# FFN order in an attention and FFN block: a gate's two parts behind the next gate's Silu, the next block's integers, projection and norms spread over both wide layers

## The chip, the cores and the metric

The kernel runs on one core of a Trainium2 chip. The metric is the device time of one execution in microseconds, the median of several runs. One further execution was taken with the hardware profiler; all views of the profile come from that one.

The engines of a core are named as the profile names them: PE (TensorE, matmuls; PEld are its weight loads), DVE (VectorE), ACT (ScalarE), POOL (GpSimd), SP (SyncE, which here only issues DMAs). They run side by side and wait for each other through semaphores.

## The reference, cut to what matters

One transformer block with the norm behind each part, on x of 4096 rows of 256 columns. The attention projects integers of 4 bits with ternary weights, and gives y; its last projection, again with integers, is computed in the kernel next to the FFN. The FFN is five linear layers with ternary weights `w` and a scale `s` for each output:

```python
def _tlin(x, w, s):
    return jnp.einsum('bsi,oi->bso', x, w) * s
# attention's end: quant4(y) @ ternary_weight(Wo_w).T
x = _layernorm(x + attention(x))
h = silu(_tlin(x, w1_w, w1_s)) * _tlin(x, w2_w, w2_s)      # 256 -> 1024, the gates
h = gelu(_tlin(h, h1_w, h1_s))                             # 1024 -> 1024, wide layer h1
h = gelu(_tlin(h, h2_w, h2_s))                             # 1024 -> 1024, wide layer h2
x = _layernorm(x + _tlin(h, w3_w, w3_s))                   # 1024 -> 256, the last layer
```

`quant4` divides each row by its largest absolute value, multiplies by 7, rounds and clips.

## The kernel before

**Stages.** A short stage quantizes x and projects it. The attention then takes some 3.1 ms of the span; its output y goes to DRAM (`y_dram`, eight blocks of 512 rows). The FFN comes last. `ffn(True)` (L718) is what runs with these weights, under `tc.manual_schedule()` (L853): each engine gets its instructions in the order in which the code writes them, and nothing is moved.

**The FFN's blocks.** The outer loop (L807) takes eight blocks b of 512 rows. Activations lie transposed, 128 features on the partitions by 512 rows. The weights are exact in fp32r, the matmuls' input type, and the activations are not; so each activation is split into two parts, its rounded value and the rest. `parts` (L725) makes them: a copy that rounds (L727, on ACT for the gates and on DVE for the wide layers) and a subtraction on DVE (L729). `product` (L733) forms 128 outputs for the 512 rows: one PSUM bank, with two matmuls (L745) for each 128 inputs.

**A block's layers**, in the order of PE:

- The gates (L810): for each o of 8, `gates` (L764) makes two products of 4 matmuls, then Silu of the first on ACT (L768), then on DVE the second product times its scale times the Silu (L770), then the two parts into `ha`.
- h1 (L820): for each o of 8, `hidden` (L776) makes one product of 16 matmuls, which reads `ha` in the order of k, both parts of each; then Gelu on ACT (L779), then the two parts into `hb`, both on DVE.
- h2 (L839): the same from `hb`.
- The last layer (L843): two products of 16 matmuls, each scaled on ACT into `fT` (L786).

**What is woven in between.** `add_up` (L788) transposes the last layer's result of block b-1 back and adds it to `xs[b-1]`. It stands behind gates 0 and 1 of block b. The closing norm of block b-1 has three steps (`layernorm_steps`, L181): `measure` (four pairs of BATCH_NORM on DVE, L189 and L190), `root` (a Sqrt on ACT, L193) and `scale` (a reciprocal and four scalings on DVE, L197 and L199). Then `store` (L799) issues the output's DMA on SP.

The next block's front (`front_steps`, L210) has seven steps. Calling it issues the load of `yb` on SP (L214). The steps are: `integers` (`quantize`, L117: eight DVE instructions on the row block), `transposed` (eight transposes on PE, L224, and a copy on ACT, L226), two projections (four matmuls on PE, L232; two DVE instructions, L241; two POOL additions, L244), and then `measure`, `root` and `scale` of that block's first norm. `transpose_x` (L756) at last transposes the normalized block, and makes its parts, for the gates of block b+1. `load_x` (L178) loads x for block b+2 on SP; three buffers of `xs` rotate, so that it goes into the buffer that `store` of block b-1 reads.

**What sets the order before.** In the gates: `measure` of block b-1 behind gate 2, and the call of `front_steps` for b+1 behind gate 4. In h1: front steps 0 to 4 behind products 0 to 4; front `root`, the closing norm's `root` and `scale`, and front `scale` behind product 5; the store behind product 6; `load_x` behind product 7. In h2: `transpose_x` behind product 1.

**Buffers.** PSUM has eight banks in one rotation (`psC`, L706), a bank for each product and each transpose. Silu and Gelu write into `gate`, three buffers in rotation, which `fT` shares. `h` has two buffers, `qtmp`, `qint`, `qT` and `yb` one each.

Of the kernel before, what the change touches and what calls it, by code (L numbers as in the profile page):

```python
# [29 lines left out]
NC = DH // P  # L30
# [7 lines left out]
def attn_ffn_kernel(  # L38
# [22 lines left out]
    nc = tc.nc  # L61
# [104 lines left out]
    def load_weights(sb, src, k0):  # L166

        n = min(sb.shape[1], 2)
        for k in range(0, sb.shape[1], n):
            nc.gpsimd.dma_start(  # L170
                out=sb[:, k : k + n, :],
                in_=src[(k0 + k) * P : (k0 + k + n) * P, :].rearrange("(k p) o -> p k o", p=P),
            )

    x_bufs = [xpool.tile([P, BT, D], F32, name=f"xs{i}") for i in range(3)]
    xs = {b: x_bufs[b % 3] for b in range(NT // BT)}

    def load_x(b):  # L178
        nc.sync.dma_start(out=xs[b], in_=x_t[:, ts(b, BT), :])
# [78 lines left out]
    with ExitStack() as actx:  # L258
# [371 lines left out]
        with tc.manual_schedule():  # L630
# [33 lines left out]
            w2_sb, h1_sb, h2_sb = [None, None], [None, None], [None, None]  # L664
# [37 lines left out]
    with ExitStack() as fctx:  # L702
        wpool2 = fctx.enter_context(tc.tile_pool(name="wpool2", bufs=1))
        hpool = fctx.enter_context(tc.tile_pool(name="hpool", bufs=2))
        tmp = fctx.enter_context(tc.tile_pool(name="tmp", bufs=2))
        psum = fctx.enter_context(tc.tile_pool(name="psC", bufs=8, space=PSUM))  # L706

        h2_sb[0] = kpool.tile([P, NC // 2, DH], F32R, name="h2a", tag="kT")
        h2_sb[1] = wpool2.tile([P, NC // 2, DH], F32R, name="h2b")
        w3_sb = wpool2.tile([P, NC, D], F32R, name="w3_sb")  # L710
        for i in range(2):
            load_weights(h2_sb[i], h2T, i * NC // 2)
        load_weights(w3_sb, w3T, 0)

        def bank(shape, dt):
            return psum.tile(shape, dt, name="ps_mm")

        def ffn(split):  # L718


            np_ = 2 if split else 1
            dt = F32R if split else F32
            nb = NT // BT

            def parts(dst, k, g, eng):  # L725

                eng(dst[:, k, 0, :], g)  # L727
                if split:
                    nc.vector.tensor_tensor(  # L729
                        dst[:, k, 1, :], g, dst[:, k, 0, :].bitcast(F32), ALU.subtract  # L730
                    )

            def product(w, o, src):  # L733
                ps = bank([P, 512], F32)
                sbs, dram_w = w
                n = dram_w.shape[0] // P
                if not split:
                    wo = tmp.tile([P, NC, P], F32, name="wo", bufs=1)[:, :n, :]
                    nc.sync.dma_start(
                        out=wo, in_=dram_w[:, ts(o, P)].rearrange("(k p) o -> p k o", p=P)  # L740
                    )
                for k in range(n):
                    sb, ks = sbs[k * len(sbs) // n], k % (n // len(sbs))
                    for i in range(np_):
                        nc.tensor.matmul(  # L745
                            ps,
                            lhsT=sb[:, ks, ts(o, P)] if split else wo[:, k, :],
                            rhs=src[:, k, i, :],
                            start=(k == 0 and i == 0),
                            stop=(k == n - 1 and i == np_ - 1),  # L750
                        )
                return ps

            xTs, fTs = {}, {}

            def transpose_x(b):  # L756
                xTs[b] = tmp.tile([P, 2, np_, BT * P], dt, name="xT", bufs=1)
                for k in range(2):
                    ps = bank([P, 512], F32)
                    for i in range(BT):  # L760
                        nc.tensor.transpose(ps[:, ts(i, P)], xs[b][:, i, ts(k, P)], ident)
                    parts(xTs[b], k, ps, nc.scalar.copy)

            def gates(b, o, ha):  # L764
                pa = product(((w1_sb,), w1T), o, xTs[b])
                pb = product((w2_sb, w2T), o, xTs[b])
                gate = tmp.tile([P, BT * P], F32, name="gate", bufs=3)
                nc.scalar.activation(gate, pa, AF.Silu, scale=scales["s1"][:, o : o + 1])  # L768
                g = gate if split else ha[:, o, 0, :]
                nc.vector.scalar_tensor_tensor(  # L770
                    g, pb, scales["s2"][:, o : o + 1], gate, ALU.mult, ALU.mult
                )
                if split:
                    parts(ha, o, g, nc.scalar.copy)

            def hidden(w, sc, o, ha, hb):  # L776
                ps = product(w, o, ha)
                g = tmp.tile([P, BT * P], F32, name="gate", bufs=3) if split else hb[:, o, 0, :]
                nc.scalar.activation(g, ps, AF.Gelu, scale=scales[sc][:, o : o + 1])  # L779
                if split:  # L780
                    parts(hb, o, g, nc.vector.tensor_copy)

            def last_layer(b, o, ha):
                ps = product(((w3_sb,), w3T), o, ha)
                fTs[o] = tmp.tile([P, BT * P], F32, name="fT", tag="gate", bufs=3)
                nc.scalar.activation(fTs[o], ps, AF.Copy, scale=scales["s3"][:, o : o + 1])  # L786

            def add_up(b, o):  # L788
                pt = bank([P, 512], F32)
                for i in range(BT):  # L790
                    nc.tensor.transpose(pt[:, ts(i, P)], fTs[o][:, ts(i, P)], ident)
                nc.vector.tensor_tensor(
                    xs[b][:, :, ts(o, P)],
                    xs[b][:, :, ts(o, P)],
                    pt.rearrange("p (i d) -> p i d", d=P),
                    ALU.add,
                )

            def store(b):  # L799
                nc.sync.dma_start(out=out_t[:, ts(b, BT), :], in_=xs[b])  # L800

            def hlayer():
                return hpool.tile([P, NC, np_, BT * P], dt, name="h")

            transpose_x(0)
            ends = None
            for b in range(nb):  # L807
                fronts = None
                ha = hlayer()
                for o in range(NC):  # L810
                    gates(b, o, ha)
                    if b and o < 2:
                        add_up(b - 1, o)
                    if b and o == 2:
                        ends = layernorm_steps(xs[b - 1])
                        ends[0]()
                    if o == 4 and b + 1 < nb:
                        fronts = front_steps(b + 1, bank)
                hb = hlayer()
                for o in range(NC):  # L820
                    hidden((h1_sb, h1T), "hs1", o, ha, hb)
                    if o < 5 and fronts:
                        fronts[o]()
                    if o == 5:

                        if fronts:
                            fronts[5]()
                        if ends:
                            ends[1]()
                            ends[2]()  # L830
                        if fronts:
                            fronts[6]()
                    if o == 6 and ends:
                        store(b - 1)
                        ends = None
                    if o == 7 and b + 2 < nb:
                        load_x(b + 2)
                ha, hb = hb, hlayer()
                for o in range(NC):  # L839
                    hidden((h2_sb, h2T), "hs2", o, ha, hb)  # L840
                    if o == 1 and b + 1 < nb:
                        transpose_x(b + 1)
                for o in range(2):  # L843
                    last_layer(b, o, hb)
            for o in range(2):
                add_up(nb - 1, o)
            for f in layernorm_steps(xs[nb - 1]):
                f()
            store(nb - 1)

        differs = nc.values_load(flag[0:1, 0:1], min_val=0, max_val=1)
        with tc.If(differs == 0) as cmp:
            with tc.manual_schedule():  # L853
                ffn(True)
        with cmp.Else():
            with tc.manual_schedule():
                ffn(False)
# [51 lines left out]
```

## Time and profile before

| What | us |
|---|---|
| median of 3 runs | 3928.08 |
| lowest and highest run | 3924.14 to 3934.04 |
| the profiled execution | 3924.8 |
| span of the profile, first to last instruction | 3923.0 |
| first matmul of the FFN's gates, from the span's start | 3179.05 |

The profile is one execution. A stretch of the trace is named by microseconds from the span's start. In the timeline each line gives the start, the duration, the engine, the line of the code, the operation with output<-input, the shape and the count of instructions merged. In brackets stands how long the engine was idle before it and what released it. A matmul's end is modelled, so successive matmuls overlap in the timeline; their starts are what to compare. The granted clock (PEclk) is a share of TensorE's full clock.

### The profile page before, as it was taken

The page shows a single profiled execution, that of the slowest core. Times are in us where ns is not written, and L with a number is a line of the kernel's source. Part 1 is how long each engine was busy: PE and PEld are TensorE (multiplying, and loading weights), DVE is VectorE, ACT ScalarE, POOL GpSimd, SP SyncE. Part 2 cuts the span into 40 slices and gives each one's busy share as a digit, 9 for nine tenths or more (in the row PEclk, how much of TensorE's full clock was granted, in tenths as well). Part 3 has the DMA queues.
Part 4 walks back from the last instruction along what each step waited for, and adds up shares of the span by engine and source line. Part 5 has one row for each costly group of instructions (what it writes and reads, how often), then busy time and mean ns, then how long its engine had stood idle before and what let it go on. Part 6 is the DMA issues. An engine that isn't in the chain of part 4 may idle for free.

```text
span 3923.0 us, 62034 instructions
## 1 busy us (share of the span) xinstructions
PE 3794.9 (97%) x25163; PEld 2161.9 (55%) x25163; DVE 3074.1 (78%) x5286; ACT 2385.0 (61%) x2694; POOL 420.6 (11%) x769
## 2 busy tenths in 40 slices
PE   4999999999999999999999999999999999999998
PEld 3555555555555555555555555555555557777776
DVE  6988888888888888888888888888888834444443
ACT  1467766766676776776666766766767753333332
POOL 6100011011100110011001100111000010000000
PEclk7799999999999999999999999999999999999999
DMA  2000000000000000000000000000100020000000
GB/s 56 1 3 2 8 8 8 8 8 8 8 8 8 8 8 8 8 8 8 8 8 8 8 8 8 8 2 24 45 2 19 2 72 17 17 17 17 17 6 12
DMA packets 59943, 49.36 MB, mean 13 GB/s; under 512 B 35232, under 2 KB 54304, under 8 KB 59648
## 3 DMA queue, kind: packets, MB, share of 16 engines
q1 hardware_dynamic: 55360, 33.11, 3.1%
q0 software_dynamic: 4288, 12.21, 1.0%
q8 instruction: 199, 3.26, 0.3%
q14 instruction: 96, 0.79, 0.1%
HBM read 36.92 MB, written 8.39 MB: 12 GB/s over the span
## 4 chain that ended last, share of the span: by engine, by line
PE 88%; DVE 8%; ACT 2%; issue 1%; DMA 0%; POOL 0%; SPq 0%; ACTq 0%; POOLq 0%; DVEq 0%
PE av L554 26%; PE sc L532 24%; PE ps L491 20%; PE ps_mm L745 13%; DVE mx L499 3%; PE ps L575 2%; DVE gate L770 1%; PE ps L519 1%; PE ps L462 1%; PE ps L416 1%; ACT gate L768 1%; DVE differ L616 0%; ACT h L727 0%; DVE qtmp L127 0%; DVE h L729 0%
## 5 line engine op out<-in xcount | busy, mean ns | idle before, releaser
L499 DVE TENSOR_REDUCE mx<-ps 128x1 f32<-128x512 f32 x4096 | 2558.6, 684 | 371.2 <-PE ps L491 353.9
L540 ACT ACTIVATE pr<-sc 128x1024 f32<-128x1024 f32 x2048 | 2012.6, 1024 | 906.5 <-PE sc L532 902.3
L491 PEld LDWEIGHTS ps<-kT,qT 64*128 64x128 f32 x4096 | 563.3, 185 | 987.1 <-DVE mx L499 636.6
L554 PE MATMUL av<-pr,v_all 128*32 128x512 f32 x8192 | 1092.8, 605 | 0.0
L491 PE MATMUL ps<-kT,qT 64*128 64x512 f32 x4096 | 1077.8, 470 | 9.2 <-DVE mx L499 8.4
L532 PE MATMUL sc<-mrow,minus 64*128 64x512 f32 x4096 | 867.5, 407 | 3.2 <-ACT pr L540 3.0
L532 PE MATMUL sc<-qT,kT 64*128 64x512 f32 x4096 | 834.2, 391 | 0.0
L532 PEld LDWEIGHTS sc<-qT,kT 64*128 64x128 f32 x4096 | 408.5, 185 | 78.7
L532 PEld LDWEIGHTS sc<-mrow,minus 64*128 64x128 f32 x4096 | 402.3, 186 | 76.7 <-ACT pr L540 19.3
L554 PEld LDWEIGHTS av<-pr,v_all 128*32 128x32 f32 x8192 | 161.6, 108 | 259.2 <-issue 255.9
L779 ACT ACTIVATE gate<-ps_mm,sc_hs 128x512 f32<-128x512 f32 x128 | 88.2, 689 | 326.3 <-PE ps_mm L745 301.7
L727 DVE CAST h<-gate 128x512 fp32r<-128x512 f32 x128 | 54.6, 427 | 266.8 <-ACT gate L779 266.6
L612 POOL CAST wround<-xs 128x1024 fp32r<-128x1024 f32 x22 | 22.9, 1039 | 1442.4 <-DMA xs<-in_h1T 512.6
L729 DVE TENSOR_TENSOR h<-gate,h 128x512 fp32r<-128x512 f32 x192 | 133.0, 692 | 48.3 <-ACT h L727 43.9
L745 PE MATMUL ps_mm<-h,h1b 128*128 128x512 f32 x512 | 140.9, 403 | 17.4 <-ACT h L727 12.7
L745 PE MATMUL ps_mm<-h,h1a 128*128 128x512 f32 x512 | 140.9, 421 | 0.0
L745 PE MATMUL ps_mm<-h,h2a 128*128 128x512 f32 x512 | 127.2, 390 | 0.0
L745 PEld LDWEIGHTS ps_mm<-h,h1b 128*128 128x128 f32 x512 | 98.2, 192 | 51.9 <-ACT h L727 20.6
L745 PE MATMUL ps_mm<-h,h2b 128*128 128x512 f32 x512 | 126.5, 389 | 0.0
L745 PEld LDWEIGHTS ps_mm<-h,h1a 128*128 128x128 f32 x512 | 102.2, 203 | 21.7
L745 PEld LDWEIGHTS ps_mm<-h,h2b 128*128 128x128 f32 x512 | 96.1, 188 | 20.0
L745 PEld LDWEIGHTS ps_mm<-h,h2a 128*128 128x128 f32 x512 | 95.6, 188 | 19.6
(147 smaller groups left out, 1978.0 us busy)
## 6 DMA issues: line engine op xcount, KB each, us to landing
xb<-in_x SPq DMA_DIRECT2D x8, 512.0 KB, 3.9
y_dram<-yu SPq DMA_DIRECT2D x64, 64.0 KB, 1.8
xs<-in_h1T SPq DMA_DIRECT2D x8, 512.0 KB, 4.0
xs<-in_h2T SPq DMA_DIRECT2D x8, 512.0 KB, 3.9
xs<-in_x SPq DMA_DIRECT2D x8, 512.0 KB, 4.2
yb<-y_dram SPq DMA_DIRECT2D x8, 512.0 KB, 5.0
out<-xs SPq DMA_DIRECT2D x8, 512.0 KB, 2.9
h1a<-in_h1T POOLq DMA_DIRECT2D x2, 1024.0 KB, 6.8
```

The lines of the kernel that those rows point to most:

```text
L416: nc.tensor.matmul(ps[:, ts(k, P)], lhsT=flat[:, ts(4 * i + k, P)], rhs=identr, start=True, stop=True,)
L462: nc.tensor.matmul(ps[:, ts(t, P)], lhsT=qq[:, t].rearrange("p j k e -> p (j k e)"), rhs=identr, start=True, stop=True,)
L491: nc.tensor.matmul(ps[j], lhsT=qTs[u][rows, ts(qt, P)], rhs=kTs[u // NQB][rows, ts(ck, 512)], start=True, stop=True,)
L499: nc.vector.tensor_reduce(mxs[u][:, qt, j, ck : ck + 1], ps[j], AX.X, ALU.max)
L532: nc.tensor.matmul(ps[:, j, :], lhsT=minus[rows, :] if first else kTs[u // NQB][rows, ts(kt, P)], rhs=mrows[u][rows, :] if first else qTs[ ...
L540: nc.scalar.activation(pr, ps, AF.Exp)
L554: nc.tensor.matmul(avs[u][strip : strip + 32, :], lhsT=v_all[:, 2 * (2 * pair + j) + a, c * (DK + 1) : c * (DK + 1) + 32], rhs=probs[s + k ...
L575: nc.tensor.matmul(y[:, t].rearrange("p j e -> p (j e)"), lhsT=ya[:, ts(t, P)], rhs=fold, start=True, stop=True,)
L727: eng(dst[:, k, 0, :], g)
L729: nc.vector.tensor_tensor(dst[:, k, 1, :], g, dst[:, k, 0, :].bitcast(F32), ALU.subtract)
L745: nc.tensor.matmul(ps, lhsT=sb[:, ks, ts(o, P)] if split else wo[:, k, :], rhs=src[:, k, i, :], start=(k == 0 and i == 0), stop=(k == n - ...
L779: nc.scalar.activation(g, ps, AF.Gelu, scale=scales[sc][:, o : o + 1])
```

## The change

`gates` no longer makes the two parts but returns the gate. The loop over the gates runs one step longer: in step o it first issues the products, Silu and multiplication of gate o, and then the parts of gate o-1.

The other steps keep their instructions and change places. `measure` of block b-1 goes from behind gate 2 to behind product 0 of h1. The front's integers go from behind product 0 of h1 to behind product 1, the transposes from product 1 to 4, the projections from 2 and 3 to 5 and 6, its `measure` from 4 to 7. Both roots and both scalings go from behind product 5 of h1 to behind product 0 of h2, and the scaling of block b+1 now stands ahead of that of b-1. The store follows there; `load_x` goes to behind product 1 of h2, and `transpose_x` from product 1 of h2 to product 3.

```diff
@@ -770,8 +770,7 @@
                 nc.vector.scalar_tensor_tensor(
                     g, pb, scales["s2"][:, o : o + 1], gate, ALU.mult, ALU.mult
                 )
-                if split:
-                    parts(ha, o, g, nc.scalar.copy)
+                return g
 
             def hidden(w, sc, o, ha, hb):
                 ps = product(w, o, ha)
@@ -803,42 +802,47 @@
                 return hpool.tile([P, NC, np_, BT * P], dt, name="h")
 
             transpose_x(0)
-            ends = None
             for b in range(nb):
-                fronts = None
+                fronts = ends = None
                 ha = hlayer()
-                for o in range(NC):
-                    gates(b, o, ha)
+                g = None
+                for o in range(NC + 1):
+
+                    held, g = g, gates(b, o, ha) if o < NC else None
+                    if o and split:
+                        parts(ha, o - 1, held, nc.scalar.copy)
                     if b and o < 2:
                         add_up(b - 1, o)
-                    if b and o == 2:
-                        ends = layernorm_steps(xs[b - 1])
-                        ends[0]()
                     if o == 4 and b + 1 < nb:
                         fronts = front_steps(b + 1, bank)
+                if b:
+                    ends = layernorm_steps(xs[b - 1])
                 hb = hlayer()
                 for o in range(NC):
                     hidden((h1_sb, h1T), "hs1", o, ha, hb)
-                    if o < 5 and fronts:
-                        fronts[o]()
-                    if o == 5:
+                    if o == 0 and ends:
+                        ends[0]()
+                    if fronts:
+                        step = {1: 0, 4: 1, 5: 2, 6: 3, 7: 4}.get(o)
+                        if step is not None:
+                            fronts[step]()
+                ha, hb = hb, hlayer()
+                for o in range(NC):
+                    hidden((h2_sb, h2T), "hs2", o, ha, hb)
+                    if o == 0:
 
                         if fronts:
                             fronts[5]()
                         if ends:
                             ends[1]()
-                            ends[2]()
                         if fronts:
                             fronts[6]()
-                    if o == 6 and ends:
-                        store(b - 1)
-                        ends = None
-                    if o == 7 and b + 2 < nb:
+                        if ends:
+                            ends[2]()
+                            store(b - 1)
+                    if o == 1 and b + 2 < nb:
                         load_x(b + 2)
-                ha, hb = hb, hlayer()
-                for o in range(NC):
-                    hidden((h2_sb, h2T), "hs2", o, ha, hb)
-                    if o == 1 and b + 1 < nb:
+                    if o == 3 and b + 1 < nb:
                         transpose_x(b + 1)
                 for o in range(2):
                     last_layer(b, o, hb)
```

## The prediction

> **What bounds the kernel now.** I read the page first, for the engine that ends last, then the stretches of one block, then that block's timeline.
>
> ```profile
> PE 3794.9 (97%) x25163; PEld 2161.9 (55%) x25163; DVE 3074.1 (78%) x5286; ACT 2385.0 (61%) x2694; POOL 420.6 (11%) x769
> ...
> PEclk7799999999999999999999999999999999999999
> ```
>
> TensorE is busy 97% of the span and nearly always at its full clock. The change touches only the FFN. Its first product starts at 3179.05 us, so it is the last 744 us of the span. There the profile's timeline shows eight blocks of some 92.25 us. Cut at the first matmul of each layer, block 3 reads (columns: stretch, length, then busy time and count of PE, PEld, DVE, ACT, POOL, then granted clock, DMA share, GB/s):
>
> ```profile
> 3454.58:3470.06 15.48, 15.48 (x73) 12.80 (x72) 9.35 (x19) 7.56 (x12) 0.00 (x0) 1.00 0.00 1
> 3470.06:3509.66 39.60, 33.95 (x145) 25.88 (x144) 23.96 (x51) 14.36 (x20) 2.87 (x4) 0.96 0.04 14
> 3509.66:3539.58 29.92, 29.92 (x137) 24.85 (x136) 10.15 (x18) 6.48 (x10) 0.00 (x0) 1.00 0.11 36
> 3539.58:3546.83 7.25, 7.25 (x33) 6.01 (x32) 1.12 (x2) 1.38 (x2) 0.00 (x0) 1.00 0.00 0
> ```
>
> These are the gates, the first wide layer (h1), the second (h2), and the last layer. Three of them have PE busy for their whole length. h1 has the same 128 large matmuls as h2, and takes 9.7 us longer, with PE idle and its clock at 0.96. So the whole loss is in h1. Its eight instances (length, PE busy and count, clock, DMA, GB/s):
>
> ```profile
> 3194.81:3232.59 37.78, 32.88 (x146) 0.95 0.04 14
> 3285.23:3325.15 39.92, 34.96 (x145) 0.91 0.04 14
> 3377.78:3417.41 39.63, 33.97 (x146) 0.96 0.04 14
> 3470.06:3509.66 39.60, 33.95 (x145) 0.96 0.04 14
> 3562.31:3601.91 39.60, 33.97 (x145) 0.96 0.04 14
> 3654.57:3694.19 39.62, 33.98 (x146) 0.96 0.04 14
> 3746.84:3786.55 39.71, 33.98 (x146) 0.96 0.04 14
> 3839.20:3873.98 34.78, 32.26 (x129) 0.95 0.05 16
> ```
>
> Block 3's timeline shows where in h1 it goes (start, duration, in brackets the idle time before and its releaser):
>
> ```profile
> 3474.09 0.62 ACT L727 CAST h<-gate 128x512 fp32r<-128x512 f32 x1 [0.83 <-DVE gate L770]
> 3474.61 0.68 ACT L768 ACTIVATE gate<-ps_mm,sc_s 128x512 f32<-128x512 f32 x1
> 3474.73 0.69 DVE L729 TENSOR_TENSOR h<-gate,h 128x512 fp32r<-128x512 f32 x1 [0.68 <-ACT h L727]
> 3474.75 0.50 PE L745 MATMUL ps_mm<-h,h1b 128*128 128x512 f32 x1 [0.82 <-ACT h L727]
> 3475.34 0.74 DVE L770 SCALAR_TENSOR_TENSOR gate<-ps_mm,sc_s,gate 128x512 f32<-128x512 f32 x1
> ...
> 3477.86 3.42 PE L745 MATMUL ps_mm<-h,h1a 128*128 128x512 f32 x8
> ...
> 3486.39 0.62 PE L224 MATMUL ps_mm<-identb,qint 128*128 128x128 bf16 x8 [3.10 <-DVE qint L131]
> ```
>
> Three losses. (a) The gates' chain runs Silu 0.68, times 0.74, copy 0.62, next Silu: 2.04 us a gate, while PE makes a gate in 1.81. ScalarE idles 0.83 before each copy, with the next Silu behind it. So the last gates' parts come late, and h1's first product waits for them matmul by matmul. (b) After that, eight matmuls take 3.42 us at a halved clock. (c) The transposes of the next block's integers wait 3.10 us for VectorE.
>
> **What the Trainium skill says.** "TensorE: Matmul & The Clock Gate", Part 1: the clock falls to half after an idle window of 3413 ns and comes back after a busy one. The trace agrees in size: in 3478 to 3480 us the granted clock was 0.52, and (b) costs 1.7 us, half of 3.41; the waits before it were broken up, though, not one solid window. The same page, on the array's architecture: ScalarE and VectorE take their queues strictly in order, and of PE only weight loads overtake. The 0.83 us before the copies agree. "ScalarE: Activation LUTs", What ACT_TABLE_LOAD costs: 1283 ns, and about as much again for a drain. The trace has 1.28 us from load to Silu and no drain after it.
>
> **The change, part by part.** First the price of h1 without waits. h2's products start every 3.63 us (3521.45, 3525.07). In block 3, h1's product 0 takes 7.80 (3470.06 to 3477.86), and from there to the transposes 8.53, product 1 and its wait. From 3486.39 to 3509.66 PE never waits: 23.27 us, six products, the transposes, two projections. So h1 needs 2 x 3.63 + 23.27 = **30.53 us**.
>
> *Gates.* Moved: copy and subtraction of gate o-1 stand behind Silu and times of gate o. No instruction is added. ScalarE now needs 0.69 + 0.62 = 1.31 us a gate and VectorE 0.74 + 0.69 = 1.43, both under PE's 1.81; the chain is gone, and PE sets the pace. New waits: Silu o waits for its first product with copy o-1 behind it, and times o for its second with subtraction o-1 behind it. I followed the queues from block 3's starts, with t = 0 at the first gate product. The second product of gate 7 ends at 15.65. Times 7 runs 15.74 to 16.48, subtraction 6 to 17.17, copy 7 to 17.12, subtraction 7 to 17.86. h1 starts at 15.48 and takes the parts in order, 0.227 a matmul: gate 6's second part at 18.43, gate 7's at 18.65 and 18.88. The thinnest margin is 1.0 us; (a) goes. Silu 7 needs the gate buffer of gate 4 (three buffers): free at 13.5, wanted at 14.8. In before, the previous block's measure (four BATCH_NORM pairs, 2.2 us of VectorE) also stood in this chain; it leaves it. With (a) gone nothing is idle before (b), and I take (b) as gone too; bounds are 0 and its full 1.7.
>
> *h1, with H its start.* Product o ends so that Gelu o starts at H + 3.63(o+1) + 0.25. Gelu 0 has its table load: its subtraction ends at H + 7.05. The measure of block b-1, moved here, runs to 9.3, cast and subtraction 1 (0.43 + 0.69) to 10.4, the integers (3481.18 to 3486.33: 5.15) to **H + 15.6**. The transposes now come after product 4, at H + 18.15: margin 2.6 us, so (c) goes. Parts 2 and 3, queued behind the integers, are done at 17.8; only h2 reads them, and Gelu 5 wants the buffer of 2 after 22. The copy of qT on ScalarE (1.0 us, behind Gelu 4) ends at 20.1, and the first projection is at 22.3. The projections' GpSimd additions (1.44 us a pair) end before the measure of b+1, which comes behind subtraction 7.
>
> *h2, with T its start.* Subtraction 7 ends at T + 2.1, wanted at T + 3.4, as before. Measure b+1 to T + 4.4. ScalarE: Gelu 0 to 4.6, table load and two roots to 6.4, table back with Gelu 1 at 8.8. VectorE: scaling of b+1 (0.18 + 1.38) to 7.7, of b-1 to 9.3. The transposes of x, moved from product 1 to product 3, come at T + 14.5: margin 6.8. No table load is added: the roots move from behind Gelu 5 of h1. SP's queue: store at T + 9.4, the load behind it once the store has landed (2.9 us), then the next yb. Both loads are wanted over 50 us later. If a cover is gone, every microsecond at h1's start costs 8 us over the blocks, at the transposes of qint or x 7.
>
> *Sum.* Blocks 1 to 6: 39.92 + 39.63 + 39.60 + 39.60 + 39.62 + 39.71 = 238.08, less 6 x 30.53: 54.9. Block 0 (no previous block): 37.78 - 30.53 = 7.25. Block 7 has no transposes or projections, so it falls to h2's own 29.01 (3873.98 to 3902.99): 5.77. The other layers stay. Together **67.9 us**. The span goes from 3923.0 to 3855.1, the profiled execution, 1.8 longer, from 3924.8 to 3856.9. That execution lies 3.3 below the median of the runs, 3928.08; taken from the median, **3860 us**.
>
> **The rivals.** *A wait comes back in part.* My margins at the gates' end and at the transposes are 1.0 and 2.6 us, put together from single durations. If VectorE is behind by as much as it was in (c), 6 x 3.1 = 19 us return: 3879. If the clock dips stay without the waits, 1.7 in seven blocks and 3.4 in block 1 return, 15 us: 3875. For: VectorE has a queue of 7.4 us (measure and integers) in front of h1's parts 2 and 3. Against: h1 gives it 30.5 us for some 20 of work. *The change doesn't do it:* the queues do not follow the written order, or PE is held by something the waits hide; 3928. Against: in the trace copy and Silu stand just as the code has them, and h2, with the same matmuls, is free of waits. *Slower:* with the pauses gone PE runs 676 us of dense 128-row matmuls, and the clock is cut under the lasting load, in the FFN alone. 676 us at clock c cost 676/c: at 0.909 the gain is used up; at 0.875 it is 3860 + 97 = 3957. From a mean below 0.90 it decides. Against: every block already runs h2, last layer and gates, 52 us, at 1.00, and attention thousands at 9 tenths or more.
>
> **How the numbers follow.** Forecast 0.80, own range 3853 to 3868, the runs of before having spread 10 us. Part of a wait back: 0.13, to 3880. No change: 0.03. Slower: 0.03. The last 0.01 lies between the part and no change. A measurement of this kernel can tell some 0.3%, 12 us, from none. So faster 0.94, same 0.03, slower 0.03. The range 3850 to 3880 leaves out under 0.1: above it only the last three cases.
>
> **What would show it.** Right: every h1 stretch near 30.5 us (the last 29.0), PE busy for its length, clock 1.00; no PE wait on the copy of L727 or on qint; ScalarE's copies right behind the next Silu; blocks of 83.2 us. Wrong: h1 over 31.5 with a wait named at h1b, at qint, at the transposes of x or at h2's last parts; gates longer than 15.5; or a clock below 1.00 where PE never waited.

## The result, and the profile after

| What | before, us | after, us |
|---|---|---|
| median of 6 runs | 3927.47 | **3854.29** |
| lowest to highest run | 3922.99 to 3934.04 | 3852.82 to 3856.44 |
| the profiled execution | 3924.8 | 3854.92 |
| its span | 3923.0 | 3853.0 |

The ratio after to before is 0.9814, with a 95% interval of 0.9801 to 0.9826: the change takes off 73 us, or 1.9%. The forecast was 3860, in a range of 3850 to 3880.

The page of the kernel after, its lines on PE:

```profile
PE 3766.5 (98%) x25163; PEld 2152.6 (56%) x25163; DVE 3069.9 (80%) x5286; ACT 2383.5 (62%) x2694; POOL 420.3 (11%) x769
...
PEclk7799999999999999999999999999999999999999
```

The counts of instructions are the same as before on every engine. PE's busy time fell by 28 us. Some of it is (b) of the prediction: the eight matmuls that took 3.42 us at the halved clock now take 1.98. Some is a matter of counting: a matmul that stood alone between two waits counted 0.50 us, with its end modelled, where matmuls in a row start 0.227 apart. The rest of the gain was idle time. These page-wide lines hardly show the change; the stretches do. Block 3 of the kernel after, cut as before into gates, h1, h2 and last layer (length, then busy time and count of PE, PEld, DVE, ACT, POOL, then granted clock, DMA share, GB/s):

```profile
3426.69:3442.17 15.48, 15.48 (x74) 12.80 (x72) 9.94 (x15) 10.55 (x17) 0.00 (x0) 1.00 0.00 1
3442.17:3472.71 30.54, 30.54 (x145) 24.84 (x144) 18.01 (x37) 8.12 (x11) 2.85 (x4) 1.00 0.00 1
3472.71:3502.63 29.92, 29.92 (x137) 24.86 (x136) 15.17 (x36) 9.53 (x14) 0.00 (x0) 1.00 0.17 53
3502.63:3509.89 7.26, 7.26 (x34) 6.01 (x32) 1.12 (x2) 1.38 (x2) 0.00 (x0) 1.00 0.00 0
```

Only the second row changed its length, from 39.60 to 30.54 us. VectorE's work moved as the code says: h1 lost 6 us of it, h2 gained 5. The h1 stretches of all eight blocks of the kernel after (length, PE busy and count, clock, DMA, GB/s):

```profile
3192.61:3223.15 30.54, 30.54 (x145) 1.00 0.06 18
3275.79:3306.34 30.55, 30.55 (x145) 1.00 0.00 1
3358.97:3389.51 30.54, 30.54 (x145) 1.00 0.00 1
3442.17:3472.71 30.54, 30.54 (x145) 1.00 0.00 1
3525.37:3555.91 30.54, 30.54 (x145) 1.00 0.00 1
3608.57:3639.11 30.54, 30.54 (x145) 1.00 0.00 1
3691.77:3722.31 30.54, 30.54 (x145) 1.00 0.00 1
3774.97:3803.98 29.01, 29.01 (x129) 1.00 0.00 1
```

PE is busy for the whole of each, at full clock. The timeline of block 3 of the kernel after, at the end of the gates and at the transposes:

```profile
3441.46 0.69 ACT L768 ACTIVATE gate<-ps_mm,sc_s 128x512 f32<-128x512 f32 x1 [0.61 <-PE ps_mm L745]
3442.05 0.61 ACT L727 CAST h<-gate 128x512 fp32r<-128x512 f32 x1
3442.17 1.98 PE L745 MATMUL ps_mm<-h,h1a 128*128 128x512 f32 x8
3442.44 0.75 DVE L770 SCALAR_TENSOR_TENSOR gate<-ps_mm,sc_s,gate 128x512 f32<-128x512 f32 x1 [0.47 <-PE ps_mm L745]
3443.11 1.47 DVE L729 TENSOR_TENSOR h<-gate,h 128x512 fp32r<-128x512 f32 x2
3443.22 0.62 ACT L727 CAST h<-gate 128x512 fp32r<-128x512 f32 x1 [0.56 <-DVE gate L770]
...
3456.75 0.69 DVE L131 TENSOR_SCALAR qint<-qtmp 128x1024 bf16<-128x1024 f32 x1
...
3460.30 0.62 PE L224 MATMUL ps_mm<-identb,qint 128*128 128x128 bf16 x8
```

Among the gates, ScalarE and VectorE now idle for PE, not for each other; only the last copy of a block still waits for VectorE (0.56). The copy of gate 6 starts right behind the Silu of gate 7, with no bracket. The last two subtractions end at 3444.58, 2.41 us into h1. The integers end at 3457.44, and PE comes to their transposes 2.86 us later, without a bracket.

PE's waits from the gates' first product to the last layer's, in the kernel before (total, times, longest):

```profile
PE ps_mm L224 <- DVE qint L131: 23.2, 7, 4.7
PE ps_mm L745 <- ACT h L727: 12.7, 21, 0.8
PE ps_mm L745 <- DVE h L729: 4.7, 21, 0.2
```

and in the kernel after:

```profile
PE ps_mm L745 <- ACT xT L727: 0.3, 1, 0.3
PE ps_mm L745 <- DVE xT L729: 0.2, 1, 0.2
```

What is left is at the very first gate. Where the 70.0 us of span went: the h1 stretches add up to 310.64 before and 242.80 after, **67.8 us**; the FFN began 3.0 earlier (3176.07, not 3179.05); and block 0's gates took 0.8 longer (16.53, not 15.76). The code ahead of the FFN is the same in both kernels. Of the 3.0, 1.3 stood already at the first matmul of the attention; most of the rest came at its end, where the halved clock lasted 3.4 us instead of 6.8. 67.8 + 3.0 - 0.8 = 70.0.

### The profile page after: what moved, and what is told of

It reads as the page before. It is cut to its first block, busy times and chain, and to the rows that moved or that the text cites. A ratio compares the mean times of both kernels' runs of the same rounds, so it can differ in the third digit from the quotient of the medians.

```text
span 3853.0 us, 62033 instructions
## 1 busy us (share of the span) xinstructions
PE 3766.5 (98%) x25163; PEld 2152.6 (56%) x25163; DVE 3069.9 (80%) x5286; ACT 2383.5 (62%) x2694; POOL 420.3 (11%) x769
## 4 chain that ended last, share of the span: by engine, by line
PE 93%; DVE 5%; ACT 1%; issue 0%; DMA 0%; POOL 0%; SPq 0%; ACTq 0%; POOLq 0%; DVEq 0%
PE av L554 26%; PE sc L532 24%; PE ps L491 21%; PE ps_mm L745 17%; DVE mx L499 3%; PE ps L575 2%; PE ps L519 1%; PE ps L462 1%; PE ps L416 1%; DVE differ L616 0%; PE ps L392 0%; ACT pr L540 0%; DMA xb<-in_x 0%; PE ps L386 0%; DVE v_all L327 0%
## 5 line engine op out<-in xcount | busy, mean ns | idle before, releaser
L745 PE MATMUL ps_mm<-h,h1a 128*128 128x512 f32 x512 | 128.9, 394 | 0.0
L745 PE MATMUL ps_mm<-h,h1b 128*128 128x512 f32 x512 | 126.5, 389 | 0.0
L770 DVE SCALAR_TENSOR_TENSOR gate<-ps_mm,sc_s,gate 128x512 f32<-128x512 f32 x64 | 48.0, 750 | 83.2 <-ACT gate L768 60.8
```

The lines of the kernel that those rows point to most:

```text
L745: nc.tensor.matmul(ps, lhsT=sb[:, ks, ts(o, P)] if split else wo[:, k, :], rhs=src[:, k, i, :], start=(k == 0 and i == 0), stop=(k == n - ...
L770: nc.vector.scalar_tensor_tensor(g, pb, scales["s2"][:, o : o + 1], gate, ALU.mult, ALU.mult)
```

## The experiments

The theory: h1 lost time at two waits of PE and at the halved clock behind them, and at nothing else. The first rival: each part of the change takes off its own wait, and they add. The second: the wide spreading, the norms and table loads out of h1, is itself worth something. In each profile the start of each product gives what was lost; "q" below is the time from h1's start to the start of the integers' transposes.

**e1, the gates' order alone.** On the kernel before:

```diff
 gates:
-                if split:
-                    parts(ha, o, g, nc.scalar.copy)
+                return g
 ffn:
-                for o in range(NC):
-                    gates(b, o, ha)
+                g = None
+                for o in range(NC + 1):
+                    held, g = g, gates(b, o, ha) if o < NC else None
+                    if o and split:
+                        parts(ha, o - 1, held, nc.scalar.copy)
```

> The kernel before with one part of the change: the gates' parts come behind the next gate's Silu; measure, integers, projections, norms and transposes stay where they were. Theory (PE waits at two places in h1, and the waits shield each other): h1's first product takes 3.63 us, also with measure still among the gates; PE then reaches the transposes of the integers at H + 7.3 while the integers end at about H + 12.2, so that the wait grows from 3.1 to about 4.9 us in seven blocks, 35 us; whether a halved clock follows this wait (1.7 us more a block, 12 in all) is open, block 0 of before had one after a wait of 4.7. Saved 68 - 35 = 33 without it, 21 with it: 3894 to 3906. Rival (each part of the change takes off its own wait): 8 x 5.9 = 47 saved, 3881.

Measured: 3902.31 us, 0.9937 of before (0.9921 to 0.9954), 24 saved. h1's first product takes 3.63 in every block, with measure still among the gates. PE comes to the transposes at 7.26 and starts them at 12.15: 4.9 us lost in seven blocks, 34. The h1 stretches are 47.2 longer than in the changed kernel in sum, so some 13 are the halved clock, which followed in all seven, in blocks 1 and 4 for two windows of 3.41 us. PE's only wait of weight in e1:

```profile
PE ps_mm L224 <- DVE qint L131: 33.2, 7, 4.7
```

and block 3's timeline:

```profile
3468.71 0.69 ACT L778 ACTIVATE gate<-ps_mm,sc_hs 128x512 f32<-128x512 f32 x1
...
3474.95 0.69 DVE L131 TENSOR_SCALAR qint<-qtmp 128x1024 bf16<-128x1024 f32 x1
...
3475.70 1.03 PE L224 MATMUL ps_mm<-identb,qint 128*128 128x128 bf16 x8 [4.74 <-DVE qint L131]
...
3476.49 3.12 PE L745 MATMUL ps_mm<-h,h1a 128*128 128x512 f32 x8
```

The total of this wait is 10 us more than in the kernel before, where the same two steps of block 3 read:

```profile
3479.40 0.69 ACT L779 ACTIVATE gate<-ps_mm,sc_hs 128x512 f32<-128x512 f32 x1
...
3485.64 0.69 DVE L131 TENSOR_SCALAR qint<-qtmp 128x1024 bf16<-128x1024 f32 x1
```

From h1's start (3470.06 before, 3463.54 in e1), the first Gelu came at 9.34 us and comes at 5.17; the integers, queued on VectorE behind its parts, ended at 16.27 and end at 12.10. Both are 4.2 earlier, as much as h1's first product is shorter (3.63, not 7.80). So the wait for the gates hid nothing of the wait for the integers: it had delayed both sides alike. What hid 1.6 us of it was the halved clock, which delayed PE alone: product 1 took 5.25 us before, and takes 3.63 in e1. In six blocks that is the 10 us. The numbers of the expectation came true, but its word that the waits shield each other holds only in this sense. The eight matmuls behind the integers' transposes take 3.12 us instead of 1.98: the clock again. The first rival's 3881 is refuted.

**e2, the spreading alone.** The changed kernel with the gates' parts put back ahead of the next gate (e1's diff, reversed).

> The kernel before with the other part alone: measure out of the gates, integers, projections and norms spread over h1 and h2 as in the changed kernel; a gate's parts again ahead of the next gate's Silu. Theory: no wait for the integers; measure is out of the gates' chain, which ends 2.1 us earlier, so that h1's first product takes about 5.7 us instead of 7.8 (4.4 in block 0). Lost against the changed kernel 7 x 2.1 + 0.8 = 15.5, so 3870 without a halved clock, 3882 with one in each of seven blocks. Rival (each part its own wait): only the 3.1 us for the integers go, 22 saved, 3905.

Measured: 3868.91 us, 0.9853 (0.9836 to 0.9869), 57 saved. No wait for integers. h1's first product takes 4.40 in block 0 and 5.67 to 5.82 in the others: 15.2 us lost over eight blocks, where 15.5 were expected. One halved clock, in block 1. PE's waits in e2:

```profile
PE ps_mm L745 <- ACT h L727: 5.7, 7, 0.8
PE ps_mm L745 <- DVE h L729: 3.1, 15, 0.2
```

These are the gates' last parts; fewer of them are waited for than before. In blocks 2 to 6 of the kernel before this product took 7.79 to 7.86; here it takes 5.67 to 5.69. So some 2.1 us of that loss came from measure on VectorE in the middle of the chain, and 2.0 from the chain itself. With the order of e1, which holds a gate's parts back, measure in the same place costs nothing.

The two halves save 24 and 57, together 81, and both at once 73; in the h1 stretches of the profiles it is 21 and 51, and 68 at once. The sum is near, but the first rival had the halves at 47 and 22. Spreading is worth more than the wait for the integers (23), because it also takes measure out of the gates' chain (2.1 in seven blocks) and leaves one of nine windows of halved clock. Each half taken alone leaves a different wait to end last.

**e3, the least spreading.** e1, and in h1 only the transposes and what follows from them later; integers, measure and h2 where they were before:

```diff
-                    if o < 5 and fronts:
-                        fronts[o]()
-                    if o == 5:
+                    if fronts:
+                        step = {0: 0, 3: 1, 4: 2, 5: 3, 6: 4}.get(o)
+                        if step is not None:
+                            fronts[step]()
+                    if o == 7:
...
-                    if o == 6 and ends:
+                    if o == 7 and ends:
                         store(b - 1)
```

> The kernel before with the gates' order of the change and the least spreading that takes the wait away: integers stay behind product 0, measure of the last block stays among the gates, transposes behind product 3, projections behind 4 and 5, the front's measure behind 6, roots, scalings and store behind 7; h2 as before. Theory (only the two waits of PE count, the rest of the moves is worth nothing): as the changed kernel, 3854 plus or minus 4, h1 near 30.5 us. Rival (the gain needs the norms and the table loads out of h1 and measure out of the gates): h1 1 to 2 us longer in each block, 3862 to 3870.

Measured: 3854.71 us, 0.9817 (0.9801 to 0.9834); the changed kernel's 3854.29 lies inside its own runs' 3853.96 to 3856.00. Seven h1 stretches of 30.54 or 30.55, one of 29.01, and no wait of PE from the gates to the last layer. So the second rival is refuted: the gates' order and the room between integers and transposes are what counts, and the other moves in h1 and h2 were worth nothing that these runs show.

**e4, the integers' margin taken away.** The changed kernel, one number:

```diff
-                        step = {1: 0, 4: 1, 5: 2, 6: 3, 7: 4}.get(o)
+                        step = {1: 0, 3: 1, 5: 2, 6: 3, 7: 4}.get(o)
```

> The changed kernel with the transposes of the integers behind product 3 of h1 instead of product 4. Theory (margin measured in the changed kernel: integers end at H + 15.3, PE is there at H + 14.5): PE waits 0.8 us in seven blocks, never long enough for a halved clock: 6 us, 3860. Rival (PE has more cover than the queues say, its transposes can slip behind work that is there): no wait, 3854.

Measured: 3860.77 us, 0.9829 (0.9813 to 0.9846), 6.5 more than the changed kernel; no run of the one reaches those of the other (from 3858.31, to 3856.44). q is 15.34 in six blocks, 0.83 behind where PE was at 14.51, and no clock fell. Block 0 shows no wait: it has no previous block, so no measure ahead of its integers. 6 x 0.83 = 5.0 us lost in the trace, in six blocks where seven were expected. The rival is refuted: there is no hidden cover.

**e5, one product earlier still.** The changed kernel again:

```diff
-                        step = {1: 0, 4: 1, 5: 2, 6: 3, 7: 4}.get(o)
+                        step = {1: 0, 2: 1, 5: 2, 6: 3, 7: 4}.get(o)
```

> The changed kernel with the transposes of the integers behind product 2 of h1. Theory: PE is there at H + 10.9, waits 4.4 us to H + 15.3 in seven blocks, 31 us. On the clock: so far a free-running window of 3.41 us that PE filled to under some 30% was always followed by a halved one, over 46% never, between both happened. A wait of 4.4 leaves one of its windows at most 36% filled, so most of the seven blocks should show a halved clock, 1.7 us each, up to 12: 3885 to 3897. Rival on the clock (it falls only after a window wholly without matmuls): a wait of 4.4 holds such a window in some 3 of 10 phases, so two blocks of seven, 3889 at the most.

Measured: 3897.31 us, 0.9923 (0.9906 to 0.9940), 0.3 above the theory's upper end. q is 14.45 in block 0 and 15.34 in the others: 3.6 and six times 4.5, 30 us of wait. The h1 stretches are 43 us longer than in the changed kernel, so 13 are the clock: it fell in all seven blocks, in blocks 0 and 5 for two windows. The windows ahead of the falls hold no matmul in three blocks and some in the other four, so the rival on the clock is refuted.

**e6, the cover in h2.** The changed kernel, transpose_x earlier:

```diff
-                    if o == 3 and b + 1 < nb:
+                    if o == 0 and b + 1 < nb:
                         transpose_x(b + 1)
```

> The changed kernel with transpose_x of the next block behind product 0 of h2 instead of product 3. Theory (the scaling of block b+1 ends at about T + 7.7, as the queues were followed): PE waits from T + 3.6 to about T + 7.7, 4.1 us in seven blocks, 29 us, and a halved clock may follow where a window is mostly idle, up to 12 more: 3883 to 3895. Rival (the cover of this step is far wider than worked out): no wait, 3854.

Measured: 3891.57 us, 0.9913 (0.9896 to 0.9929), inside the theory's range. But the wait was built otherwise than expected. Block 3's timeline in e6:

```profile
3493.68 1.38 DVE L199 TENSOR_SCALAR xs<-xs,mv,rs 128x256 f32<-128x256 f32 x4
3494.15 2.30 PE L761 MATMUL ps_mm<-ident,xs 128*128 128x128 f32 x8 [3.11 <-DVE xs L199]
```

PE starts 0.47 us behind the first of four scalings, not behind the last: each transpose waits for the 128 rows that it reads (the weight loads wait again for L199 at 3494.47, 3494.79 and 3495.11). So the wait is 3.3 us, and then the transposes and the first product behind them run slowly, held by the next scalings and by a halved clock in each of the seven blocks. Together h2 takes 5.2 to 5.6 us longer than in the changed kernel.

## Why the prediction was right

**What bounds it.** "The whole loss is in h1" is what the stretches and e3 show. h1 without waits was put at 30.53 us from block 3 of before; it is 30.54 or 30.55 in seven blocks, and 29.01 in the eighth as stated. The sum of 67.9 was measured as 67.8. The other 5 us of the medians' 73 are in no step of the sum: 2 are from the start of the FFN and block 0's gates in the profiled executions, and 3 stand between the medians and the two profiled executions, the one before being a low one of its kernel, the one after not. That is mostly why the forecast of 3860 lay 6 us too high although its sum came true.

**The gates.** The queues as followed by hand put the last subtraction at 2.38 us into h1, and it ended at 2.41; its matmul comes at 3.40, so the margin of 1.0 us was real. Measure was said to leave the chain; e2 gives its price there, 2.1 us a block, and e1 shows that under the new order it would have been free.

**The integers.** Put at H + 15.6, measured H + 15.3; the margin of 2.6 was 2.9. e4 and e5 take it away one product at a time, and the wait appears at the size that the queues give.

**The clock.** (b) was taken as gone with (a), and is gone. The trace of before had left open why it fell at waits that were broken up. In all eight profiles every stretch of the recorded clock but the last is a whole multiple of 3.41 us, so I cut the FFN into windows of that length in step with the recorded falls, and filled each with its matmuls from their starts (an estimate: 0.227 us for one of 512 columns, 0.11 and 0.054 for transposes of 128 columns in fp32 and bf16, as they follow each other at full clock). Of the windows at full clock, 24 were filled to 27% or less, and after every one the clock fell. Of 1536 filled to 46% or more, none was followed by a fall. Of 14 between, six were. So a window need not be without matmuls: one three quarters empty was enough each time, and a somewhat fuller one at times; the Trainium skill, "TensorE: Matmul & The Clock Gate", Part 1, speaks of an idle window, and here the measurement decides.

**Where it was off.** "If a cover is gone, every microsecond costs 7" (at the transposes) holds only for short waits: e4's 0.8 us cost its own length, while e5's waits of 3.6 to 4.5 cost 43 us in sum for 30 of wait, since the clock fell behind each. And the scaling of x was treated as one step, where its readers take it by 128 rows: e6's transposes began at T + 6.9, 0.8 before the scaling's stated end at T + 7.7, though the later ones then waited for the rest. Neither reached the forecast, since nothing waits in those places.

**The rivals.** A wait back in part: none came. The clock dips staying without the waits: no fall in the FFN of the changed kernel behind its first gates. The clock cut under lasting load: 1.00 in every block behind the first gates, over 650 us of dense matmuls.

Left open: the changed kernel's runs spread 3.6 us, those of before 11. Waits that vary from run to run are an obvious guess, but e1 and e5, which wait and lose the clock in seven blocks, spread 1.8 and 3.2 over four runs each, and no run here was made to tell.

## What to carry to other kernels

Cut the trace into stages and look for one that has a twin without the loss. The twin's spacing, with what the stage itself does where it never waits, prices the stage without waits: 30.53 us here, and 30.54 measured. When two waits follow each other on the engine that sets the end, follow the queues to the second before counting a gain from the first. If the first delays the data of the second as much as the engine that waits for it, removing it leaves the second as it was; what delays that engine alone, as the halved clock did here, comes back as wait. Between the step that makes data and the step that reads it, leave as many products as the maker's queue takes: three were enough for the integers here and two were not where measure stood ahead of them, and e3 shows that spreading the other steps more widely brought nothing.

## What was not expected of the hardware

In these profiles TensorE's clock halved after every window of 3.41 us that was filled to 27% or less by the estimate above, and after some filled to between 27 and 43%, not only after an idle one: before this change five matmuls of 0.227 us in a window did not keep it up in five blocks. So e5's waits of 3.6 to 4.5 us cost 6.2 each on average, and e4's of 0.8 cost 0.8.
